# Interleaving projection tiles with sign-product tiles in the last stage of a convolution kernel

## The chip, the cores and the metric

The kernel runs on one core of a Trainium2 chip. The metric is the device time of one execution in microseconds (us), the median of several runs. The engines are named as the profile names them: PE is TensorE (matmuls; PEld are its weight loads), DVE is VectorE, ACT is ScalarE, POOL is GpSimd, SP is SyncE, which here only issues transfers.

## The reference

The input `x` has 384 channels of 192 x 192 pixels in float32. Two layers follow one another, each with a residual. Cut to what matters:

```python
# layer 0
x = x + conv0(gn(x))        # conv0: 1x1 conv to q, k, v; 2x2 max pool; 3x3 depthwise conv;
                            # channel attention (8 heads, four top-k softmaxes); gelu; repeat 2x2;
out = einsum('bchw,oc->bohw', out, w_proj) + b_proj          # the projection, last step of conv0
# layer 1
xb = sign(gn(x)); wb = sign(weight)
shifted = take_along_axis(pad(xb), ...)                      # each channel shifted by -3..3 pixels
x = x + einsum('bchw,oc->bohw', shifted, wb) + bias          # the sign products
```

The normalization of layer 1 needs only the mean of each group of channels, since a sign doesn't depend on the scale. That mean is worked out before the last stage.

## The kernel before, in words

The image is cut into 24 units of 8 rows (`NU`, `UR`). A unit of `x` is a tile `xt` of 128 partitions x 3 channel tiles (`CT`) x 1536 pixels, 2304 KB. Earlier stages take statistics over all units, form q and k and their products, then v, the attention and the gelu; the result for all units lies in six `chunk` tiles of SBUF, at half the resolution in both directions.

The last stage, which starts at line 665, does for each unit, in an order given by the list `order`:

- **The projection**, `projected(ps, u, m)`: for one channel tile `m`, three fp32 matmuls (line 559) of the unit's part of `chunk` by `wpr`, which the profile shows as six passes, into a PSUM tile `yps` (128 x 384); then two additions on DVE (line 568), which add each value to its 2 x 2 pixels of `xt`. `summed(i)` does all three channel tiles of the unit `order[i]`, and issues the load of another unit when a `chunk` tile has been used up.
- **The signs**, `signed(i)`: six sign activations on ACT (line 723; two halves of three channel tiles), each followed by small copies on POOL (`moved`) that shift some channels. The signs lie in one of three fp8 tiles `signs`. In between, ACT issues the store of unit i - 2 (`stored`, line 764), and SP the load of a later unit into the same `xt` (line 768), which waits until that store has landed.
- **The sign products**, `finished(i)`: for each channel tile two PSUM tiles `l1ps` [...], each filled by six fp8 matmuls (line 743) and read by one DVE addition into `xt` (line 751).

PSUM holds two `yps` tiles and three `l1ps` tiles (line 667). The stage runs under `tc.manual_schedule()`: every engine executes its instructions in the order in which the code issues them. The order is the loop at its end:

```python
for i in range(NU):
    if i == 0:
        summed(3)
    elif i > 1 and i + 2 < NU:
        summed(i + 2)
    finished(i)
    if i + 2 < NU:
        signed(i + 2)
```

So in the steps i = 2 to 21, called units below, PE does the three projection tiles of the unit two ahead, and then all six `l1ps` tiles of unit i; DVE does six additions of line 568, then six of line 751.

Of the kernel before, what the change touches and what calls it, by code (L numbers as in the profile page):

```python
# [10 lines left out]
F32 = mybir.dt.float32  # L11
# [5 lines left out]
ALU = mybir.AluOpType  # L17
# [3 lines left out]
P = 128  # L21
C = 384
CT = C // P
# [8 lines left out]
UR = 8  # L32
NU = H // UR
UPX = UR * W
PR = UR // 2
PPX = PR * WP
# [11 lines left out]
SAT = [16 + t * STEP + t - SHIFT // 2 for t in range(CT)]  # L48
# [99 lines left out]
def conv_preact_kernel(ctx: ExitStack, tc: tile.TileContext, a: dict, out: bass.AP):  # L148
    nc = tc.nc
    xv = a["x"].rearrange("u t p n -> u p t n")  # L150
    ov = out.rearrange("u t p n -> u p t n")
# [12 lines left out]
    bpr, bl1, bq, bdw, temp = (parts[i] for i in ("b_proj", "bias", "b_qkv", "b_dw", "temp"))  # L164
# [6 lines left out]
    wb = const.tile([P, CT, C], F8, name="wb")  # L171
# [5 lines left out]
    def unit(u, pool=big, parts=1):  # L177
        xt = pool.tile([P, CT, UPX], F32, name="xt", tag="big")
        n = CT // parts
        for t in range(0, CT, n):  # L180
            nc.sync.dma_start(xt[:, t : t + n], xv[u][:, t : t + n])
        return xt
# [37 lines left out]
    with tc.tile_pool(name="p1", bufs=1, side="right") as p1, tc.tile_pool(name="p1ps", bufs=2, space=PSUM) as psp:  # L220
# [5 lines left out]
        for i in range(NU):  # L226
            u = NU - 1 - i
            xt = unit(u, parts=CT if u in (0, NU - 1) else 1)
# [22 lines left out]
            if u == NU // 2:  # L251

                for m in range(3):
                    ps = psp.tile([NG, C], F32, name="wgps")
# [15 lines left out]
        ps = psp.tile([NG, 2], F32, name="gsps")  # L270
# [10 lines left out]
        ps = psp.tile([P, CT, 2], F32, name="spread")  # L281
# [9 lines left out]
        ps = psp.tile([P, NM], F32, name="bqps")  # L291
# [61 lines left out]
    with tc.tile_pool(name="p2w", bufs=1, side="right") as wp, tc.tile_pool(  # L353
        name="p2t", bufs=2, side="right"
# [65 lines left out]
        for u in range(NU):  # L420
# [4 lines left out]
            xt = kept.pop(u)  # L425
            lo, hi = rows(u)
            n = hi - lo + 1
# [122 lines left out]
    def opened(name, bufs, **kw):  # L550
        return end.enter_context(tc.tile_pool(name=name, bufs=bufs, reuse_waits="tile", **kw))

    def projected(ps, u, m):

        xt = kept[u]
        o = chunk[u // UC][:, :, u % UC * PPX : (u % UC + 1) * PPX]
        x5 = xt.rearrange("p t (i a j b) -> p t a i j b", a=2, b=2, j=WP)
        for t in range(CT):
            nc.tensor.matmul(  # L559
                ps,  # L560
                wpr[:, t, m * P : (m + 1) * P],
                o[:, t, :],
                start=(t == 0),
                stop=(t == CT - 1),
            )
        yb = ps.rearrange("p (i j) -> p i j", j=WP).unsqueeze(3).to_broadcast([P, PR, WP, 2])
        for r in range(2):
            nc.vector.scalar_tensor_tensor(x5[:, m, r], yb, bpr[:, m : m + 1], x5[:, m, r], ALU.add, ALU.add)  # L568

    chunk = []  # L570
    with ExitStack() as vs:
# [34 lines left out]
        for u in range(NU):  # L606
            xt = kept.pop(NU + u) if NU + u in kept else unit(u)
# [9 lines left out]
            for m in range(CT):  # L617
                parts = []
                for c in range(first // CR, last // CR + 1):
                    r0, r1 = max(first, c * CR), min(last, c * CR + CR - 1)  # L620
# [4 lines left out]
                if u == 0 and m == 1:  # L625
                    gathered()
                    po = vs.enter_context(tc.tile_pool(name="p4o", bufs=NP, space=PSUM))
                    psp = vs.enter_context(tc.tile_pool(name="p3ps", bufs=1, space=PSUM))
# [13 lines left out]
        with tc.manual_schedule():  # L642
# [10 lines left out]
            ps = psp.tile([P, P], F32, name="p3ps")[:NG, :1]  # L653
# [4 lines left out]
            ps = psp.tile([P, P], F32, name="p3ps")[:, :CT].unsqueeze(2)  # L658
# [6 lines left out]
    with end:  # L665
        more, sp = opened("p5x1", 1), opened("p5s", 1)
        pyp, psp = opened("p5py", 2, space=PSUM), opened("p5ps", 3, space=PSUM)
        signs = [sp.tile([P, SALL], F8, name=f"signs{i}") for i in range(NSIGN)]

        rest = [sp.tile([P, SLEN], F8, name=f"rest{i}") for i in range(2)]  # L670
        assert SALL % 4 == LEAD % 4 == PITCH % 4 == W % 4 == 0
        for ts in (*signs, *rest):
            nc.gpsimd.memset(ts.bitcast(F32), 0.0)

        def rows_of(ts, p, at=0, pitch=PITCH, n=W):
            return ts[p, at : at + UR * pitch].rearrange("p (r w) -> p r w", w=pitch)[:, :, :n]

        order = [u for c in reversed(range(NCH)) for u in reversed(range(c * UC, (c + 1) * UC))]
        ahead = [*FIRST, NU - 1, *(u for u in order if u // UC == FIRST[0] // UC and u not in FIRST)]
        order = [*ahead, *(u for u in order if u not in ahead)]  # L680
        left = [UC] * NCH
        todo = [u for u in order if u not in kept]

        def summed(i):

            u = order[i]
            if i >= len(FIRST):
                for m in range(CT):
                    projected(pyp.tile([P, PPX], F32, name="yps"), u, m)
            left[u // UC] -= 1  # L690
            if not left[u // UC] and todo:
                v = todo.pop(0)
                kept[v] = unit(v)

        def moved(sg, t, h):

            d, n = OTHER[t][h]
            p = slice(h * HALF + REST, h * HALF + REST + n)
            src, to = SAT[t] - HSHIFT[t][h], SAT[t] - d
            by = rest[t % 2]  # L700
            nc.gpsimd.tensor_copy(
                rows_of(by.bitcast(I32), p, 0, PITCH // 4, W // 4),
                rows_of(sg.bitcast(I32), p, src // 4, PITCH // 4, W // 4),
            )
            if d:

                assert to % 4 == 0
                nc.gpsimd.tensor_copy(sg.bitcast(I32)[p, to // 4 : (to + SLEN) // 4], by.bitcast(I32)[p])
            elif to % 2 == 0:
                nc.gpsimd.tensor_copy(  # L710
                    rows_of(sg.bitcast(U16), p, to // 2, PITCH // 2, W // 2),
                    rows_of(by.bitcast(U16), p, 0, PITCH // 2, W // 2),
                )
            else:
                nc.gpsimd.tensor_copy(rows_of(sg, p, to), rows_of(by, p))  # L715

        def signed(i):

            xt, sg = kept[order[i]], signs[i % NSIGN]
            for k in range(2 * CT):  # L720
                t, h = divmod(k, 2)
                p = slice(h * HALF, (h + 1) * HALF)
                nc.scalar.activation(  # L723
                    rows_of(sg, p, SAT[t] - HSHIFT[t][h]),
                    xt[p, t, :].rearrange("p (r w) -> p r w", w=W),
                    AF.Sign,
                    bias=nmean1[p, t : t + 1],
                    saturate=False,
                )
                moved(sg, t, h)  # L730
                if i > 1 and k == min(2 * (i - 2), CT):
                    stored(i - 2)

        def finished(i):

            u = order[i]
            xt, sg = kept[u], signs[i % NSIGN]
            for m in range(CT):
                for r0 in range(0, UR, 4):
                    ps = psp.tile([P, 2, 512], F32, name="l1ps")  # L740
                    for j in range(2):
                        for t in range(CT):
                            nc.tensor.matmul(  # L743
                                ps[:, j, : 2 * W],
                                wb[:, t, m * P : (m + 1) * P],
                                rows_of(sg, slice(0, P), SAT[t])[:, r0 + 2 * j : r0 + 2 * j + 2],
                                start=(t == 0),
                                stop=(t == CT - 1),
                            )
                    blk = xt[:, m, r0 * W : (r0 + 4) * W].rearrange("p (j n) -> p j n", j=2)  # L750
                    nc.vector.scalar_tensor_tensor(  # L751
                        blk, ps[:, :, : 2 * W], bl1[:, m : m + 1], blk, ALU.add, ALU.add
                    )
                if i + 2 >= NU:
                    nc.sync.dma_start(ov[u, :, m], xt[:, m])

        def stored(i):


            u = order[i]  # L760
            xt = kept.pop(u)
            n = 1 if i < CT else CT
            for t in range(0, CT, n):
                nc.scalar.dma_start(ov[u][:, t : t + n], xt[:, t : t + n])
            if todo:
                v = todo.pop(0)
                for t in range(0, CT, n):
                    nc.sync.dma_start(xt[:, t : t + n], xv[v][:, t : t + n])
                kept[v] = xt

        with tc.manual_schedule():
            v = todo.pop(0)
            kept[v] = unit(v, more, parts=CT)
            for i in range(3):
                summed(i)
                if i < 2:
                    signed(i)
            for i in range(NU):
                if i == 0:
                    summed(3)  # L780
                elif i > 1 and i + 2 < NU:
                    summed(i + 2)
                finished(i)
                if i + 2 < NU:
                    signed(i + 2)

# [71 lines left out]
```

## Time and profile before

| | |
|---|---|
| time, median of 3 runs | 2287.42 us (2287.11 to 2288.5) |
| span of the profiled execution | 2286.9 us |
| PE busy | 2101.7 us, 92% |
| DVE busy | 1903.2 us, 83% |
| ACT busy | 819.4 us, 36% |
| POOL busy | 211.4 us, 9% |
| projection passes in the last stage (line 559 into `yps`) | 396, 136.5 us busy |
| sign products (line 743) | 864, 150.6 us busy |
| additions of line 568 into `xt` from `yps` | 132, 127.9 us busy |
| additions of line 751 | 144, 135.6 us busy |
| signs (line 723) | 144, 226.5 us busy |
| loads into `xt`, 2304 KB each | 12.8 us from issue to landing (median) |
| stores from `xt`, 2304 KB each | 14.4 us from issue to landing (median) |

The profile is of one execution. Busy times are sums over a group of instructions of one line; instructions of one engine overlap at their ends, so that a group's count times the length of one is more than its busy time. In lines of the chain of waits and of the timeline the first number is the start in us from the beginning of the span, the second the length in us, and x12 means twelve instructions joined. A note in brackets, as [0.19 <-DVE xt L568], says how long the engine was idle before and what ended that.

### The profile page before, as it was taken

What the parts mean: (1) busy time and instruction counts of PE and PEld (TensorE: products, weight loads), DVE (VectorE), ACT (ScalarE), POOL (GpSimd) and SP (SyncE); (2) the same over time, 40 slices, a digit from 0 to 9 for tenths busy, and PEclk for the clock granted to TensorE, in tenths of its full rate; (3) what the DMA queues carried; (4) which work ended last, traced back from release to release, by engine and by line L of the source; (5) the groups of instructions that cost most, each with busy time, mean ns of one, the idle gap of its engine ahead of it and who ended that gap; (6) DMA issues with size and microseconds to landing.
All of it is one profiled execution on the core that took longest, in us unless ns stands there. A gap on an engine that the chain in (4) does not pass through costs nothing.

```text
span 2286.9 us, 19474 instructions
## 1 busy us (share of the span) xinstructions
PE 2101.7 (92%) x6135; PEld 993.8 (43%) x6135; DVE 1903.2 (83%) x3269; ACT 819.4 (36%) x1418; POOL 211.4 (9%) x338
## 2 busy tenths in 40 slices
PE   1029999999999999999999979999999999999998
PEld 0014444444444444444444434444444444455554
DVE  4657888888888888888888878986787887889998
ACT  5532222222222222222222212225323233487775
POOL 0000000000000000000000000000000000286674
PEclk7559999999999999999999989999999999999999
DMA  9962222232222232222232222104221212289996
GB/s 398 417 261 60 66 63 70 66 102 69 66 63 71 66 101 70 66 64 70 68 99 70 66 48 83 42 18 189 83 83 67 99 42 83 83 333 404 423 412 248
DMA packets 208727, 300.30 MB, mean 131 GB/s; under 512 B 162000, under 2 KB 164848, under 8 KB 208624
## 3 DMA queue, kind: packets, MB, share of 16 engines
q1 hardware_dynamic: 197936, 243.46, 30.8%
q10 hardware_dynamic: 10688, 55.61, 6.0%
q8 instruction: 48, 0.79, 0.1%
q14 instruction: 55, 0.45, 0.1%
HBM read 213.68 MB, written 56.62 MB: 118 GB/s over the span
## 4 chain that ended last, share of the span: by engine, by line
PE 78%; DVE 11%; DMA 7%; ACT 2%; issue 1%; SPq 1%; ACTq 0%; POOL 0%; POOLq 0%; DVEq 0%
PE qkv L321 65%; DMA xt<-in_x_dram 7%; PE l1ps L743 5%; DVE chunk L344 4%; PE yps L559 3%; PE gram L412 3%; DVE pooled L328 2%; PE ops L594 2%; DVE xt L568 2%; DVE dw L344 1%; DVE stats L248 1%; DMA out_dram<-xt 1%; ACT signs L723 1%; SPq L401 0%; DVE xt L751 0%
## 5 line engine op out<-in xcount | busy, mean ns | idle before, releaser
L321 PE MATMUL qkv<-xt,wq 128*128 128x512 f32 x3888 | 1684.0, 594 | 0.3 <-DVE small L294 0.3
L321 PEld LDWEIGHTS qkv<-xt,wq 128*128 128x128 f32 x3888 | 737.1, 191 | 921.6 <-issue 825.1
L344 DVE SCALAR_TENSOR_TENSOR dw<-pooled,small,dw 128x384 f32<-128x384 f32 (+2 forms) x1152 | 709.2, 616 | 118.8 <-ACT dw L342 93.7
L328 DVE TENSOR_REDUCE pooled<-qkv 128x128 f32<-128x512 f32 x648 | 442.7, 684 | 73.6 <-PE qkv L321 73.1
L344 DVE SCALAR_TENSOR_TENSOR chunk<-pooled,small,chunk 128x384 f32<-128x384 f32 (+3 forms) x696 | 370.5, 546 | 74.7 <-ACT chunk L342 57.3
L346 ACT COPY pooled<-pooled 128x196 f32<-128x196 f32 x207 | 73.7, 356 | 764.5 <-DVE dw L344 543.0
L335 ACT ACTIVATE pooled<-pooled,small 128x384 f32<-128x384 f32 x216 | 133.0, 616 | 409.6 <-DVE pooled L328 402.0
L723 ACT ACTIVATE signs<-xt,nmean 64x1536 fp8e4<-64x1536 f32 x144 | 226.5, 1573 | 61.5 <-PE yps L559 50.3
L743 PE MATMUL l1ps<-signs,wb 128*128 128x384 fp8e4 x864 | 150.6, 329 | 6.2 <-POOL signs L715 4.5
L568 DVE SCALAR_TENSOR_TENSOR xt<-yps,small,xt 128x768 f32<-128x768 f32 x132 | 127.9, 1013 | 23.8 <-PE yps L559 19.6
L559 PE MATMUL yps<-chunk,wpr 128*128 128x384 f32 x396 | 136.5, 490 | 5.5 <-DVE xt L568 5.5
L751 DVE SCALAR_TENSOR_TENSOR xt<-l1ps,small,xt 128x768 f32<-128x768 f32 x144 | 135.6, 1008 | 6.3 <-ACT signs L723 3.6
L248 DVE BATCH_NORM_STATS2 stats<-xt 128x6 f32<-128x512 f32 x144 | 87.2, 675 | 60.4 <-DMA xt<-in_x_dram 60.4
L198 PE MATMUL gsps<-sums,small 128*32 128x2 f32 x6 | 0.5, 196 | 128.5 <-DVE sums L269 128.5
L433 ACT ACTIVATE sq<-dw 128x384 bf16<-128x384 f32 (+2 forms) x144 | 75.3, 523 | 117.0 <-DVE dw L344 117.0
L743 PEld LDWEIGHTS <-wb 128*128 128x128 fp8e4 x864 | 84.1, 97 | 74.0 <-issue 16.3
L302 POOL MEMSET pooled<- 128x196 f32 x9 | 2.4, 265 | 1173.3 <-DVE dw L344 1155.8
L342 ACT ACTIVATE dw<-pooled,small 128x384 f32<-128x384 f32 (+2 forms) x144 | 100.5, 698 | 2.3
L559 PEld LDWEIGHTS yps<-chunk,wpr 128*128 128x128 f32 x396 | 72.6, 190 | 61.0 <-PE yps L559 16.4
L239 ACT ACTIVATE junk<-xt 128x1536 bf16<-128x1536 f32 x48 | 71.1, 1482 | 52.3 <-DMA xt<-in_x_dram 51.1
L383 DVE STREAM_TRANSPOSE blocks<-dw 128x384 f32<-128x384 f32 (+1 forms) x144 | 82.0, 570 | 3.4
L412 PE MATMUL gram<-room 128*128 128x160 f32 (+3 forms) x438 | 68.1, 309 | 15.4 <-DMA room<-blocks 15.4
(117 smaller groups left out, 640.1 us busy)
## 6 DMA issues: line engine op xcount, KB each, us to landing
xt<-in_x_dram SPq DMA_DIRECT2D x83, 2304.0 KB, 12.8
out_dram<-xt ACTq DMA_DIRECT2D x19, 2304.0 KB, 14.4
room<-blocks SPq DMA_DIRECT2D x736, 36.0 KB, 2.0
xt<-in_x_dram SPq DMA_DIRECT2D x18, 768.0 KB, 8.0
out_dram<-xt ACTq DMA_DIRECT2D x9, 768.0 KB, 7.9
out_dram<-xt SPq DMA_DIRECT2D x6, 768.0 KB, 6.6
wq<-in_w_qkvT_dram ACTq DMA_DIRECT2D x1, 1728.0 KB, 15.0
room<-blocks SPq DMA_DIRECT2D x32, 48.0 KB, 2.1
```

The costliest lines, as they stand in the source:

```text
L248: nc.vector.bn_stats(stats[b][:, t, at : at + 6], xt[:, t, j * 512 : (j + 1) * 512])
L321: nc.tensor.matmul(ps, wq[:, t, m * P : (m + 1) * P], x4[:, t, r0 : r0 + nr, c0 : c0 + ncol], start=(t == 0), stop=(t == CT - 1),)
L328: nc.vector.tensor_reduce(pl[:, 2 + r0 // 2 : 2 + (r0 + nr) // 2, 1 + c0 // 2 : 1 + (c0 + ncol) // 2], ps.rearrange("p (i a j b) -> p i j ...
L335: nc.scalar.activation(new, new, AF.Identity, bias=bq[:, m : m + 1])
L342: nc.scalar.activation(acc2, src, AF.Identity, bias=bdw[:, m : m + 1], scale=wdw[:, m, 0:1])
L344: nc.vector.scalar_tensor_tensor(acc2, src, wdw[:, m, k : k + 1], acc2, ALU.mult, ALU.add)
L412: nc.tensor.matmul(gram[t][:, : BN[t] * B], q[:L, t, i], k[:L, B0[t] : B0[t] + BN[t], i], start=u == 0 and i == 0, stop=u == NU - 1 and i ...
L559: nc.tensor.matmul(ps, wpr[:, t, m * P : (m + 1) * P], o[:, t, :], start=(t == 0), stop=(t == CT - 1),)
L568: nc.vector.scalar_tensor_tensor(x5[:, m, r], yb, bpr[:, m : m + 1], x5[:, m, r], ALU.add, ALU.add)
L723: nc.scalar.activation(rows_of(sg, p, SAT[t] - HSHIFT[t][h]), xt[p, t, :].rearrange("p (r w) -> p r w", w=W), AF.Sign, bias=nmean1[p, t : ...
L743: nc.tensor.matmul(ps[:, j, : 2 * W], wb[:, t, m * P : (m + 1) * P], rows_of(sg, slice(0, P), SAT[t])[:, r0 + 2 * j : r0 + 2 * j + 2], sta ...
L751: nc.vector.scalar_tensor_tensor(blk, ps[:, :, : 2 * W], bl1[:, m : m + 1], blk, ALU.add, ALU.add)
```

## The change

`summed` and `finished` are given the channel tile `m`, and the loop calls them in turn: one projection tile of the unit two ahead, then the two `l1ps` tiles of one channel tile of the present unit, and so three times. It is meant to keep PE from waiting for a `yps` tile: with two such tiles, three projection tiles in a row need one of them twice. The instructions and their number are the same; only the order on PE and DVE, and with it the time at which each unit's sums and signs are ready, is another. The first two units and the last two, which have no projection beside them, keep their order. The diff, cut to its core:

```diff
-        def summed(i):
+        def summed(i, m):
             u = order[i]
             if i >= len(FIRST):
-                for m in range(CT):
-                    projected(pyp.tile([P, PPX], F32, name="yps"), u, m)
+                projected(pyp.tile([P, PPX], F32, name="yps"), u, m)
+            if m < CT - 1:
+                return
             left[u // UC] -= 1
...
-        def finished(i):
+        def finished(i, m):
             u = order[i]
             xt, sg = kept[u], signs[i % NSIGN]
-            for m in range(CT):
-                for r0 in range(0, UR, 4):
+            for r0 in range(0, UR, 4):
...
-            for i in range(3):
-                summed(i)
+            for i in range(4):
+                for m in range(CT):
+                    summed(i, m)
                 if i < 2:
                     signed(i)
             for i in range(NU):
-                if i == 0:
-                    summed(3)
-                elif i > 1 and i + 2 < NU:
-                    summed(i + 2)
-                finished(i)
+                for m in range(CT):
+                    if 1 < i < NU - 2:
+                        summed(i + 2, m)
+                    finished(i, m)
                 if i + 2 < NU:
                     signed(i + 2)
```

More of the change, by code (lines that the diff above doesn't have):

```diff
@@ L732, in signed @@
                     stored(i - 2)
-        def finished(i):
+        def finished(i, m):
             u = order[i]
             xt, sg = kept[u], signs[i % NSIGN]
-            for m in range(CT):
-                for r0 in range(0, UR, 4):
[L740 to L755, printed above, removed]
+            for r0 in range(0, UR, 4):
+                ps = psp.tile([P, 2, 512], F32, name="l1ps")
+                for j in range(2):
+                    for t in range(CT):
+                        nc.tensor.matmul(
+                            ps[:, j, : 2 * W],
+                            wb[:, t, m * P : (m + 1) * P],
+                            rows_of(sg, slice(0, P), SAT[t])[:, r0 + 2 * j : r0 + 2 * j + 2],
+                            start=(t == 0),
+                            stop=(t == CT - 1),
+                        )
+                blk = xt[:, m, r0 * W : (r0 + 4) * W].rearrange("p (j n) -> p j n", j=2)
+                nc.vector.scalar_tensor_tensor(
+                    blk, ps[:, :, : 2 * W], bl1[:, m : m + 1], blk, ALU.add, ALU.add
+                )
+            if i + 2 >= NU:
+                nc.sync.dma_start(ov[u, :, m], xt[:, m])
         def stored(i):
```

## The prediction

> **What bounds the kernel now.** I read three views in this order: the span in 40 slices, to find the stage that the change touches; the chain of waits there; the timeline of single engines over one unit. Only the last 300 us matter: the change moves nothing before about 2017 us. The stage's stretches, with busy time (and instructions) of PE, PEld, DVE, ACT and POOL, then clock, DMA share and GB/s:
>
> ```profile
> 2030.00:2083.00 53.00, 50.65 (x224) 28.51 (x223) 46.11 (x49) 41.66 (x27) 37.35 (x54) 1.00 0.95 369
> 2083.00:2255.00 172.00, 168.03 (x753) 94.16 (x751) 159.07 (x168) 131.19 (x84) 116.13 (x168) 1.00 0.92 383
> 2255.00:2287.00 32.00, 22.62 (x122) 12.65 (x120) 22.77 (x25) 12.59 (x8) 11.27 (x16) 0.94 0.72 295
> ```
>
> PE and DVE are both almost always busy, so neither share tells which sets the pace. The chain of waits does (start, us, what):
>
> ```profile
> 2142.78 1.95 PE yps L559 x6
> 2144.75 1.96 DVE xt L568 x2
> 2146.70 0.14 issue
> 2146.84 2.17 PE yps L559 x6
> 2149.01 2.95 PE l1ps L743 x18
> 2151.97 3.11 PE l1ps L743 x18
> 2155.09 1.95 PE yps L559 x6
> 2157.06 1.95 DVE xt L568 x2
> ```
>
> It is a loop that repeats from 2083 to 2267 us. All steps are PE, but for one: after two projection tiles PE must wait until DVE has read the first, because only two `yps` tiles exist. The timeline of PE, then of DVE, in the same unit:
>
> ```profile
> 2142.61 4.03 PE L559 MATMUL yps<-chunk,wpr 128*128 128x384 f32 x12
> 2146.84 2.17 PE L559 MATMUL yps<-chunk,wpr 128*128 128x384 f32 x6 [0.19 <-DVE xt L568]
> 2148.85 6.24 PE L743 MATMUL l1ps<-signs,wb 128*128 128x384 fp8e4 x36
> 2154.92 4.03 PE L559 MATMUL yps<-chunk,wpr 128*128 128x384 f32 x12
> ...
> 2144.75 3.88 DVE L568 SCALAR_TENSOR_TENSOR xt<-yps,small,xt 128x768 f32<-128x768 f32 x4 [0.51 <-PE yps L559]
> 2149.05 1.94 DVE L568 SCALAR_TENSOR_TENSOR xt<-yps,small,xt 128x768 f32<-128x768 f32 x2 [0.43 <-PE yps L559]
> 2150.91 5.63 DVE L751 SCALAR_TENSOR_TENSOR xt<-l1ps,small,xt 128x768 f32<-128x768 f32 x6
> 2157.06 3.88 DVE L568 SCALAR_TENSOR_TENSOR xt<-yps,small,xt 128x768 f32<-128x768 f32 x4 [0.52 <-PE yps L559]
> ```
>
> The period is 2154.92 - 2142.61 = 12.31 us. Three waits of the stage are to be kept in mind (us in all, times, longest):
>
> ```profile
> ACT signs L723 <- PE yps L559: 50.3, 18, 3.8
> PE yps L559 <- DVE xt L568: 5.5, 22, 1.4
> DVE xt L568 <- DMA xt<-in_x_dram: 4.2, 3, 1.9
> ```
>
> [...] the six L751 follow one another at (5.63 - 1.005) / 5 = 925 ns[...] the stage reaches 424 in its busiest stretches.
>
> **The change part by part.**
>
> 1. Bare work of PE per unit. A projection pass takes (4.03 - 0.49) / 11 = 0.322 us (x12, one taking 0.49), so 18 take 5.80. A sign product takes 2.95 / 18 = 0.164, so 36 take 5.90. Together 11.70; the period has 0.61 more. Where: twelve passes should end at 2142.61 + 3.87 = 2146.48, and the thirteenth starts at 2146.84 (0.36); its six last 2148.85 - 2146.84 = 2.01 and not 1.93 (0.08); the 36 products last 2154.92 - 2148.85 = 6.07 (0.17). The last loss lies between products 18 and 19 (the second 18 take 3.11, not 2.95): product 19 opens the fourth `l1ps` tile, whose buffer DVE frees when its first L751, begun at 2150.91, is through.
>
> 2. What the new order removes. It alternates one projection tile (1.93) with two `l1ps` tiles (1.97): 3.90 us per channel tile. The `yps` tile needed next was filled two channel tiles (7.8 us) earlier, and in the built program the later projections carry no wait at all. DVE needs 2 x 0.934 + 2 x 0.925 = 3.72 for the same channel tile, less than PE, so it lags by one tile's work and no more: the first L751 of a channel tile ends about 5 us after that channel tile's start on PE, and its buffer is wanted again three `l1ps` tiles later, at about 7. So all of 0.61 should go: PE's period becomes 11.70.
>
> 3. What it adds. Six changes between fp32 and fp8 per unit in place of two. Before shows each kind once per unit: from the last projection pass to the first product 0.32, from the last product to the first pass 0.16, each no more than the instruction itself. I take zero; the upper bound is 0.08 (the restart of step 1) for four more, 0.3. For DVE a wait at each of six changes: an L568 that starts after idling costs some 0.08 more (it takes 1.018 where the next follows after 0.934); 3.72 + 0.08 is still under 3.90. What stands behind a waiting DVE instruction is the next pair of additions, and PE has two to three filled tiles of room.
>
> 4. What moves: the third projection tile of unit i+2 is added by DVE about 4 us later. Signs of channel tile 2 stand on ACT behind the store of unit i, which waits for the last L751 of unit i anyway; signs of tile 1 have their input 6 us into the unit, and ACT comes to them at about 7 (0.5 for the store's issue, then four signs of 1.6). ACT does six signs (9.44) per unit and waits 2.75, so about 2 of slack remain. The products need the signs a unit later. Chunk buffers are freed by PE 4 us later, but the two loads I checked (2029.28 and 2071.20) stood in SP's queue behind another load until 3 us and more after that. Cost: nothing, hidden in ACT's and SP's waiting.
>
> 5. How many units. Units 2 to 7 run while the DMA engines are full (share 0.99 to 1.01 but for 2045 to 2060, where it is 0.83): loads set the pace, DVE waiting for `xt` at units 3, 4 and 7. The new order helps at unit 3: DVE waited 1.9 us there for the last third of a load with sum and product of the first thirds undone, and now does these first. Its store is issued up to 1.9 us earlier, into the slack stretch, and the loads that follow may gain as much. After the last stall (2083.21) DVE takes 11.2 instead of 12.3 us for unit 7, as PE has run ahead. Between 0.9 and 3.0; I take 2.0.
>
> 6. From the first projection addition of unit 8 (2095.52) to that of unit 21 are 13 periods: 13 x 0.61 = 7.9. The last addition of unit 21 comes 0.2 sooner within its unit. The tail (signs and products of the last two units, last stores) is the same. Sum 2.0 + 7.9 + 0.2 = 10.1; 2287.4 - 10.1 = 2277.3 us.
>
> **The rivals.**
>
> A, the above: 2277.3, chance 0.56.
>
> B, PE doesn't get all: the 0.17 and 0.08 stay in another form, or changes of type cost up to 0.3 per unit. Period 11.95 to 12.05: 13 x 0.3 = 3.9, with 1.5 from the early units: 5.4, so 2282.0. For it: only two changes per unit were ever seen, and DVE has 0.1 us of slack per channel tile. Against it: those two cost nothing. 0.24.
>
> C, the loads take over. One unit moves 4.72 MB, at 424 GB/s 11.13 us, only 0.57 under the new period, and chunk buffers bring two more loads between 2110 and 2175. Should the loads hold the pace at 12.31 until they end at about 2225, the gain is some five units of 0.61 and one of unit 7: 4, so about 2283.4 to 2286. Against it: load for unit 8's projection lands, by the bytes of the load queue, at about 2092, needed at 2094.5; three units later the slack is 9 us and grows. 0.14.
>
> D, slower: the later signs become the bound. If ACT's chain (store issue, two signs, wait for tile 1, two signs, wait for the store) took 0.25 longer than a period of 12.31, 20 units would lose 5: 2292. Against it: 2 us of slack, worked out in 4. 0.06.
>
> **How the numbers follow.** A is the likeliest: 2277.3. Below it only the 3.0 of step 5 lies and some luck: 2275.5. Above, the range takes in B and the near end of C: 2283.0. C's rest (0.08) and D (0.06) stay out, with a little of A's lower side. Faster by over 0.2% means under 2282.8: A, three quarters or more of B, a little of C, 0.80; slower is D, 0.06; same the rest, 0.14.
>
> **What would show it.** Right: PE's timeline shows 6 passes, 12 products, 6 passes, with no idle note from DVE; the period from 2095 on is 11.7; the entry "PE yps <- DVE xt" shrinks from 22 times to none or a few; DVE's waits for PE become many short ones. B: period of 12 with PE idle put down to issue or DVE. C: more than three DVE waits for `xt` loads. D: PE or PEld waiting for ACT signs or POOL beyond the three of before. Wrong altogether: the period stays at 12.3, which would mean that PE's bare work is more than 11.70.

## The result, and the profile after

| | before | after |
|---|---|---|
| time, median of 4 runs | 2287.96 us (2287.11 to 2289.1) | 2275.48 us (2274.21 to 2276.92) |
| ratio, 95% interval | | 0.9945 [0.9928, 0.9963] |
| span of the profiled execution | 2286.9 us | 2274.4 us |

The change takes 12.5 us away. The forecast was 10.1, and the time lies 0.02 us below the low end of its range. Single executions of after lie between 2274.2 and 2276.9, so that on which side of that end their median falls is chance; what has to be explained is the 2.4 us between 10.1 and 12.5. The interval of the ratio alone (a gain of 8.5 to 16.5 us) can't tell these two apart; the traces, unit by unit, can. The chain of waits of after, in a unit of the same stretch as shown for before (start, length, what):

```profile
2141.77 1.97 PE l1ps L743 x12
2143.73 1.94 PE yps L559 x6
2145.67 1.97 PE l1ps L743 x12
```

There is nothing but PE in it: the steps "issue" and "DVE xt" are gone. PE's timeline of after, then DVE's:

```profile
2139.67 2.10 PE L559 MATMUL yps<-chunk,wpr 128*128 128x384 f32 x6
2141.60 2.13 PE L743 MATMUL l1ps<-signs,wb 128*128 128x384 fp8e4 x12
2143.57 2.10 PE L559 MATMUL yps<-chunk,wpr 128*128 128x384 f32 x6
...
2149.41 2.13 PE L743 MATMUL l1ps<-signs,wb 128*128 128x384 fp8e4 x12
2151.38 2.10 PE L559 MATMUL yps<-chunk,wpr 128*128 128x384 f32 x6
...
2141.80 1.94 DVE L568 SCALAR_TENSOR_TENSOR xt<-yps,small,xt 128x768 f32<-128x768 f32 x2
2143.66 1.94 DVE L751 SCALAR_TENSOR_TENSOR xt<-l1ps,small,xt 128x768 f32<-128x768 f32 x2
2145.71 1.94 DVE L568 SCALAR_TENSOR_TENSOR xt<-yps,small,xt 128x768 f32<-128x768 f32 x2
```

A unit lasts 2151.38 - 2139.67 = 11.71 us in place of 12.31. No line of PE carries an idle note. DVE starts the two additions of a projection tile every 3.91 us (2145.71 - 2141.80) and is idle for some 0.1 of it. The waits of after (engine, tile and line, what it waited for: us in all, times, longest):

```profile
ACT signs L724 <- PE yps L559: 23.6, 11, 2.1
PE l1ps L743 <- POOL signs L716: 4.8, 2, 3.5
DVE xt L568 <- DMA xt<-in_x_dram: 4.7, 2, 2.6
DVE xt L568 <- PE yps L559: 2.8, 5, 0.9
PE yps L559 <- DVE xt L568: 0.4, 2, 0.2
```

PE's wait for a free `yps` went from 22 times and 5.5 us to twice and 0.4. ACT's wait for projections halved (50.3 to 23.6 us): with PE quicker, the slack of ACT is smaller but still there. DVE's waits for loads are 4.7 us as against 4.2; what of them reaches PE is told below.

**Where the 12.5 us lie.** Unit 1's last addition ends at 2018.0 us in both traces (2018.01 and 2018.06). From there, by DVE's timelines (the first row gives a moment, the others lengths, all in us):

| stretch | before | after | gain | forecast |
|---|---|---|---|---|
| up to the first projection addition of unit 8, at | 2095.52 | 2091.82 | 3.7 | 2.0 |
| from there to that of unit 21 | 160.00 | 151.46 | 8.5 | 7.9 |
| from there to the end of unit 21 | 11.8 | 11.6 | 0.2 | 0.2 |
| from the end of unit 21 to the end of the kernel | 19.55 | 19.55 | 0 | 0 |

In this pair of traces, then, the early units gave nearly twice what the forecast put down. How that looks on DVE, in after, around the last wait for a load:

```profile
2069.41 1.94 DVE L568 SCALAR_TENSOR_TENSOR xt<-yps,small,xt 128x768 f32<-128x768 f32 x2 [2.55 <-DMA xt<-in_x_dram]
2071.27 1.93 DVE L751 SCALAR_TENSOR_TENSOR xt<-l1ps,small,xt 128x768 f32<-128x768 f32 x2
...
2080.71 1.94 DVE L568 SCALAR_TENSOR_TENSOR xt<-yps,small,xt 128x768 f32<-128x768 f32 x2
...
2091.82 1.93 DVE L568 SCALAR_TENSOR_TENSOR xt<-yps,small,xt 128x768 f32<-128x768 f32 x2
...
2102.92 1.94 DVE L568 SCALAR_TENSOR_TENSOR xt<-yps,small,xt 128x768 f32<-128x768 f32 x2
```

Unit 6 begins at 2069.41 after a stall of 2.55 us. The next three units start 11.30, 11.11 and 11.10 later each: DVE's own pace (12 additions of 0.925 are 11.10), below PE's 11.71. PE had filled tiles ahead during the stall, and for some three units DVE works these off. In before, units 5 and 6 and all from 8 on took 12.31 from end to end (unit 4, 12.41). There PE could not stay ahead, since it waited for DVE once per unit.

How much of a stall reaches PE, which sets the pace, can be read from PE's lines. In after, behind DVE's stalls of 2.19 us (at 2044) and 2.55 us:

```profile
2046.19 2.44 PE L743 MATMUL l1ps<-signs,wb 128*128 128x384 fp8e4 x12
2072.33 1.15 PE L743 MATMUL l1ps<-signs,wb 128*128 128x384 fp8e4 x6 [1.26 <-DVE xt L751]
```

Twelve products last 2.13 elsewhere, so that the first stall cost PE 0.3; the second cost 1.26 of idling and the 0.16 by which products otherwise overlap the matmul before them (2.13 against the 1.97 of the chain), 1.4 together. In before, DVE's stalls were 1.88, 0.62 and 1.70, and PE's notes are these, where an undisturbed unit has 0.19 in the place of the last two:

```profile
2039.91 3.12 PE L743 MATMUL l1ps<-signs,wb 128*128 128x384 fp8e4 x18 [1.46 <-DVE xt L751]
2047.19 2.17 PE L559 MATMUL yps<-chunk,wpr 128*128 128x384 f32 x6 [0.29 <-DVE xt L568]
2085.30 2.17 PE L559 MATMUL yps<-chunk,wpr 128*128 128x384 f32 x6 [1.38 <-DVE xt L568]
```

So in before a stall came through to PE but for some 0.4 or 0.5 us (1.46 of 1.88, 0.10 of 0.62, 1.19 of 1.70); in after, 1.1 and 1.9 us did not come through. In all, waits for loads cost PE 2.7 us in before and 1.7 in after, and the lengths of units 2 to 20 give the same two sums. The new order thus takes up a part of each stall.

What the DMA engines did meanwhile, in the stretches 2018 to 2078 and 2083 to 2245 (from:to, length, busy of PE, PEld, DVE, ACT, POOL, then clock, DMA share and GB/s), of after:

```profile
2018.00:2078.00 60.00, 58.59 (x270) 33.88 (x269) 53.70 (x59) 52.22 (x34) 46.60 (x67) 1.00 0.96 378
2083.00:2245.00 162.00, 162.00 (x751) 94.51 (x750) 158.12 (x168) 131.60 (x84) 115.87 (x168) 1.00 0.97 403
```

and of before:

```profile
2018.00:2078.00 60.00, 57.45 (x256) 32.06 (x255) 53.26 (x58) 51.15 (x34) 45.26 (x65) 1.00 0.95 360
2083.00:2245.00 162.00, 158.23 (x705) 88.50 (x703) 149.50 (x158) 123.49 (x80) 107.96 (x157) 1.00 0.95 396
```

In the early stretch the share hardly moved (0.95 to 0.96), and yet 5% more was carried (360 to 378 GB/s). Before alone shows the same already, in two stretches with a share of 1.01 and 1.02:

```profile
2071.00:2083.30 12.30, 12.10 (x55) 6.79 (x54) 10.18 (x12) 9.48 (x7) 8.29 (x12) 1.00 1.01 386
2107.80:2120.10 12.30, 12.10 (x55) 6.78 (x55) 11.37 (x12) 9.44 (x6) 8.30 (x12) 1.00 1.02 424
```

So a share near 1 stood beside 386 GB/s and beside 424 alike, and didn't show how much was still to be had. From 2083 to 2245 PE of after is busy all of the time.

### The profile page after: what moved, and what is told of

It is laid out like the page before. It is cut to its first block, busy times and chain, and to the rows that moved or that the text cites. A ratio compares the mean times of both kernels' runs of the same rounds, so it can differ in the third digit from the quotient of the medians.

```text
span 2274.4 us, 19469 instructions
## 1 busy us (share of the span) xinstructions
PE 2093.8 (92%) x6135; PEld 995.7 (44%) x6135; DVE 1902.4 (84%) x3269; ACT 819.4 (36%) x1418; POOL 211.3 (9%) x338
## 4 chain that ended last, share of the span: by engine, by line
PE 79%; DVE 11%; DMA 6%; ACT 2%; issue 1%; SPq 1%; ACTq 0%; POOL 0%; POOLq 0%; DVEq 0%
PE qkv L321 64%; PE l1ps L743 6%; DMA xt<-in_x_dram 5%; PE yps L559 5%; DVE chunk L344 5%; PE gram L412 3%; DVE pooled L328 2%; PE ops L594 2%; DVE dw L344 1%; DVE stats L248 1%; ACT signs L724 1%; ACT chunk L342 0%; ACT pooled L335 0%; SPq L401 0%; DVE xt L751 0%
## 5 line engine op out<-in xcount | busy, mean ns | idle before, releaser
L724 ACT ACTIVATE signs<-xt,nmean 64x1536 fp8e4<-64x1536 f32 x144 | 226.5, 1573 | 49.0 <-PE yps L559 23.6
```

The costliest lines, as they stand in the source:

```text
L724: nc.scalar.activation(rows_of(sg, p, SAT[t] - HSHIFT[t][h]), xt[p, t, :].rearrange("p (r w) -> p r w", w=W), AF.Sign, bias=nmean1[p, t : ...
```

## The experiments

Each is a small edit of the last stage. Medians are given with the ratio to the kernel before and its 95% interval; "gain" is the difference from the median of before on the same chip (2287.6 to 2288.1). Single executions of one kernel differ by 2 us and more: in the traces, unit 1 ends between 2015.7 and 2018.1 us (but for the kernel with one `yps` tile), before most of the edits have any effect, and the early waits for loads scatter too.

**Which units gave it.** The alternation is kept only where `c` holds; elsewhere the three projection tiles go first as before:

```diff
-                for m in range(CT):
-                    if 1 < i < NU - 2:
-                        summed(i + 2, m)
-                    finished(i, m)
+                ahead = i + 2 if 1 < i < NU - 2 else None
+                if ahead and not c:
+                    for m in range(CT):
+                        summed(ahead, m)
+                for m in range(CT):
+                    if ahead and c:
+                        summed(ahead, m)
+                    finished(i, m)
```

`c` is `i > 7` in the first, `i < 8` in the second, `i == 3` in the third and `4 <= i < 8` in the fourth.

Late units alone:

> Alternates from unit 8 on only; units 2 to 7 keep the old order. Theory (two separate gains: 0.6 us in each steady unit from PE's waits for PSUM tiles, and some 3.7 us in the load-paced units 2 to 7): unit 8 begins where it began before (first projection addition at about 2095.5 us), period 11.7 from there, gain 8.0 to 8.5, so about 2279.3. Rival (the steady units are the whole gain, the early 3.7 being chance in the transfers): about 2275.5, as the full change.

Early units alone:

> Alternates in units 2 to 7 only; from unit 8 on the old order. Theory: first projection addition of unit 8 at about 2091.8 us, then periods of 12.3; gain 3.7, so about 2284. Rival (all of the gain in the steady units): no gain, 2287.5. The two gains of this run and of the one with the late units should add up to the 12.4 us of the full change.

Unit 3 alone, the prediction's own reason for the gain before unit 8:

> Alternates in unit 3 only. If the early gain comes from unit 3 alone (DVE no longer idles 1.9 us for the last third of a load, its store goes out 2 us sooner): 3 to 3.7 us gained by unit 8, about 2284. If it comes from the load-paced units together, each issuing its store somewhat sooner: 0.5 to 1.5 gained, about 2286.5.

Units 4 to 7 alone:

> Alternates in units 4 to 7 only, that is without units 2 and 3. Theory A (after a wait for a load, DVE, which needs only 11.1 us per unit, catches up with PE, which has run ahead into the PSUM tiles; that happens in units 4 to 7 alone): nearly the whole early gain, 3 to 3.5 us, about 2284.5. Theory B (each of the six units simply saves 0.6 us, the loads following suit): 4 x 0.6 = 2.4, about 2285.6. The prediction's own reason (unit 3's earlier store): nothing, 2288.

| alternating in | median us | ratio | gain |
|---|---|---|---|
| units above 7 | 2279.79 | 0.9963 [0.9951, 0.9976] | 8.3 |
| units below 8 | 2284.6 | 0.9986 [0.9979, 0.9993] | 3.5 |
| unit 3 | 2288.07 | 1.0002 [0.9994, 1.001] | 0 |
| units 4 to 7 | 2285.08 | 0.9988 [0.998, 0.9996] | 2.9 |

The two halves come out at 8.3 and 3.5, near what the traces of before and after had (8.5 + 0.2 and 3.7), and add up to 11.8 of the 12.5. The interval of the early half is wide: 1.6 to 4.8 us. By itself it doesn't exclude the 2.0 of the forecast. The traces help here: from the end of unit 1 to that of unit 7, the two with the old order in these units (before and the kernel with late units alone) take 77.0 and 78.0 us; the three with the new order (after, early units alone, and the kernel at the end of this section that stores unit 21 by channel tile) take 73.9, 74.9 and 74.5. Every one of the three is more than 2.0 us below either of the two, and the means lie 3.1 apart. After unit 7, another 0.6 and more comes in while DVE still catches up.

Unit 3 alone gives nothing in its median (interval -2.3 to 1.4 us). In its trace, its store went out earlier by some 1.6 to 2 us, but half of that went into a new wait at unit 4 (1.43 us), and the wait at unit 7 stayed (1.69, in before 1.70). So the reason that step 5 gave for most of its term, unit 3 and the loads behind its store, is not the cause. Units 4 to 7 alone bring 2.9 (interval 0.9 to 4.6), which lies between what the two theories of that run expected and doesn't decide between them; it does show a gain in these units, which the forecast held to be paced by loads.

**Which wait was removed.** Two projection tiles, then four `l1ps` tiles, then the third projection tile, then two `l1ps` tiles:

```diff
-                    if 1 < i < NU - 2:
-                        summed(i + 2, m)
+                    if ahead and m != 1:
+                        for k in (0, 1) if m == 0 else (2,):
+                            summed(ahead, k)
                     finished(i, m)
```

> All units from 2 to 21, but in the order two projection tiles, two channel tiles of sign products, one projection tile, one channel tile of products. Theory (only a third projection tile in a row has to wait, as there are two yps tiles): no wait for yps, the period at most 0.1 us over 11.7, so 2275.5 to 2277. Rival (PE and DVE must alternate tile by tile to keep step): part of the 0.6 us comes back, a period near 12, about 2280.

2280.4 us, 0.9966 [0.9954, 0.9979]: a gain of 7.7, not the full one that was expected; the time is the one that the rival of that run named, but with a shorter period than its "near 12". PE's timeline of this kernel has no wait for `yps`:

```profile
2146.32 2.10 PE L559 MATMUL yps<-chunk,wpr 128*128 128x384 f32 x6
2148.26 2.13 PE L743 MATMUL l1ps<-signs,wb 128*128 128x384 fp8e4 x12
2150.23 4.03 PE L559 MATMUL yps<-chunk,wpr 128*128 128x384 f32 x12
2154.10 4.27 PE L743 MATMUL l1ps<-signs,wb 128*128 128x384 fp8e4 x24
2158.20 2.10 PE L559 MATMUL yps<-chunk,wpr 128*128 128x384 f32 x6
```

Its period is 2158.20 - 2146.32 = 11.88. The chain of waits shows the 0.17 that stayed:

```profile
2142.38 2.95 PE l1ps L743 x18
2145.34 0.01 issue
2145.34 1.15 PE l1ps L743 x6
```

18 products take 2.95, so six take 0.98, and the six after the break, which open the fourth `l1ps` tile, take 1.15. This splits the 0.60 us per unit (12.31 - 11.71): 12.31 - 11.88 = 0.43 was the wait for `yps` with its restart, 11.88 - 11.71 = 0.17 the wait for the fourth `l1ps` tile in a row. The change removes both.

The change with one `yps` tile in place of two:

```diff
-        pyp, psp = opened("p5py", 2, space=PSUM), opened("p5ps", 3, space=PSUM)
+        pyp, psp = opened("p5py", 1, space=PSUM), opened("p5ps", 3, space=PSUM)
```

> The full change with one yps tile in place of two: the wait that the change removed, put back. A projection tile can then begin only when DVE has read the last one, 2.13 + 1.87 + 0.15 = 4.15 us after that began, against 3.90: period 12.45, 0.15 over the old order's, so about 2289. If the wait for yps were not what the change removed, the time would stay at 2275.5.

2314.79 us, 1.0113 [1.01, 1.0127]: 26.9 us slower than before, where about 2289 had been expected. The chain of waits of this kernel, and a line of PE's timeline:

```profile
2154.99 2.19 PE yps L559 x6
2157.18 0.03 issue
2157.20 1.95 DVE xt L568 x2
2159.16 0.14 issue
2159.29 2.19 PE yps L559 x6
...
2154.99 2.17 PE L559 MATMUL yps<-chunk,wpr 128*128 128x384 f32 x6 [0.16 <-DVE xt L568]
```

The tile is filled (2.19), read by DVE (1.95), and the hand-overs cost 0.03 and 0.14: 4.30 us per channel tile, 12.90 per unit. The two `l1ps` tiles that stand between fit into the reading and cost nothing. 4.15 had been expected; each part came out a little longer than put down (2.19 for 2.13, 1.95 for 1.87, 0.17 for 0.15). The two profiled executions lie 22.7 us apart, and this is where: unit 1 ends 8.7 later than in before, since six projection tiles go in a row ahead of unit 0's products; unit 2 takes 18.16 in place of 12.71; and the 19 units from 3 on take 12.90 each, 245.1 in place of 236.6. The last term would be 11 but for before's waits for loads, of which this kernel has none. The expectation had counted the period alone. The other 4 us of the medians are in no trace.

The change with two `l1ps` tiles in place of three, by the same line (3 to 2):

> The full change with two l1ps tiles in place of three. The steady period stays 11.7, since with alternation a buffer is wanted again 3.9 us after it was filled and DVE is through with it after about 3.2. PE can run ahead of a DVE that waits for a load by one tile (1 us) less: theory A loses some 0.5 to 1 us of the early gain, 2276 to 2276.5; theory B loses nothing, 2275.5. If the third tile were needed in the steady units: period over 12, 2280 or more.

2275.78 us, 0.9948 [0.9934, 0.9961], the same as the change; the period in its trace is 11.71. With one `yps` tile the period of the alternation was 12.90, with two it is 11.71, and here the third `l1ps` tile brought nothing (one alone was not tried). The loss that one theory expected from a smaller lead of PE was not seen in the time, but at 0.5 to 1 us it would hide in the spread of these runs (2274.1 to 2277.4). PE's idle notes fit a smaller lead: behind DVE's stalls of 1.80 and 1.05 us, PE idled 0.74 and 0.38 here.

**What the loads took.** In both orders, a load that follows a store brings only channel tile 0 of its unit; two thirds of these loads are left out:

```diff
-                for t in range(0, CT, n):
-                    nc.sync.dma_start(xt[:, t : t + n], xv[v][:, t : t + n])
+                nc.sync.dma_start(xt[:, :1], xv[v][:, :1])
```

In the order of before:

> The old order, but a load that follows a store brings only the first of three channel tiles (the output is then not that of the reference; the work of the engines is the same). No DVE wait for a load: units 2 to 7 at 12.3 like the others, 73.9 us from the end of unit 1 to that of unit 7 in place of 77.0; about 2285, the loads' waits costing 3 us in the old order.

In the order of the change:

> The full change with the same light loads (the same part is left out). Units 2 to 7 at 11.7: 70.3 us to the end of unit 7. Theory (the waits for loads cost about as much in either order, as loads follow stores and stores follow the units): 12 us less than the old order with light loads, about 2273, and 2.5 to 3 less than the full change. The prediction's reading (units 2 to 7 are paced by the DMA engines, so that the new order gains only a part of its 0.6 there): the waits would cost more in the new order, 4.5 or more, about 2271 or less.

2285.04 us, 0.9986 [0.998, 0.9993], for the old order and 2273.33 us, 0.9934 [0.9922, 0.9946], for the new. In neither trace does DVE wait for a load in this stage; unit 2 takes 12.7 in both, and every unit from 3 to 21 takes 12.31 or 11.71. The two medians differ by 11.7 us; 19 units of 0.60 are 11.4. With whole loads they differ by 12.5. So loads cost 3.0 us in the old order (2288.0 - 2285.0) and about 2.2 in the new (2275.5 - 2273.3, from two chips); by the traces, 2.7 and 1.7. They took nothing of the gain, where the prediction's reading would have had them cost 4.5 or more in the new order. This is what the forecast had wrong.

**Stores, the order within a pair, and the end.** The products of a channel tile before the projection tile:

```diff
-                        summed(i + 2, m)
                     finished(i, m)
+                    if 1 < i < NU - 2:
+                        summed(i + 2, m)
```

> Alternates, but the products of a channel tile go ahead of the projection of the same channel tile. The period is the same 11.7; loads get 2 us more before they are needed, the last unit's signs come 2 us later, so that the tail's wait for them grows by 1 to 2. Together 2275 to 2277. If the order within a pair mattered for the steady units (DVE waiting longer for PE): 2278 or more.

2273.55 us, 0.9934 [0.9922, 0.9947]: 1.9 under the change, at the same period of 11.71, and below the 2275 to 2277 expected. Its waits have one for a load, not two:

```profile
DVE xt L568 <- DMA xt<-in_x_dram: 1.5, 1, 1.5
```

Whether this comes from the store, which is ready one projection tile sooner, was tried by putting that store behind the signs of the next two units, products first as above:

```diff
-                if i > 1 and k == min(2 * (i - 2), CT):
+                if i > 1 and k == (2 * CT - 1 if i > 4 else min(2 * (i - 2), CT)):
```

> Products first, as in the run before, but the store of a unit is issued behind all six signs, not behind the fourth: some 5 us later. Theory (the time at which a unit's store is issued sets when the load behind it lands, and so the waits for loads): 5 to 8 us of new waits in units 4 to 10, 2279 to 2282. If the moment of the store doesn't matter, the DMA engines being full anyway: 2273.5 as before.

2275.03 us, 0.9944 [0.9932, 0.9957], not the 2279 to 2282 expected. The stores went out 1.2 to 2.6 us later, not 5, and unit 7 ended as soon as without the edit (71.15 and 71.19 us after unit 1). What is lost (1.5 in the medians, 2.3 in this part of the traces) is lost behind unit 21, whose store is late too: 21.81 us are left from there to the end, and 19.55 with products first. A store's moment, by some 2 us, set no load's wait here.

The last stage's end was tried next: products first up to unit 20, projection first for unit 21, whose store alone goes behind the signs.

```diff
-                if i > 1 and k == min(2 * (i - 2), CT):
+                if i > 1 and k == (2 * CT - 1 if i == NU - 1 else min(2 * (i - 2), CT)):
...
+                    if ahead == NU - 1:
+                        summed(ahead, m)
                     finished(i, m)
+                    if ahead and ahead < NU - 1:
+                        summed(ahead, m)
```

> Products first in units 2 to 20, projection first in unit 21, and in the last signs the store behind the sixth sign, so that the last unit's signs come 2 us sooner. The tail's waits of PE (1.0) and DVE (0.8) before the last products go: about 2272.7, 0.8 under products first throughout. If the tail waits for something else: 2273.5.

2275.03 us, 0.9943 [0.993, 0.9955]: the 2272.7 expected was missed by 2.3. The last additions came 1.2 us sooner than in the kernel with products first, and yet the end came later (1.5 in the medians, 1.75 in the traces), as the store of unit 21 went out later. The issue of that store here:

```profile
2252.80 0.38 ACTq L764 DMA_DIRECT2D out_dram<-xt  x1
```

and with products first:

```profile
2251.05 0.38 ACTq L764 DMA_DIRECT2D out_dram<-xt  x1
```

From 2252.80 on the DMA engines of this kernel are busy to the end while PE is not (columns as above):

```profile
2252.80:2269.80 17.00, 10.08 (x62) 5.72 (x60) 11.13 (x12) 1.40 (x1) 2.84 (x4) 0.91 0.96 393
```

17 us at 393 GB/s are 6.7 MB: nearly all of the three units that are then still to be stored (7.1 MB). And from the end of unit 21 to the end of the kernel it is 19.55 or 19.56 us with products first, here, and in the change, though the last addition comes 14.3, 11.2 and 12.6 us after unit 21. Behind unit 21, then, transfers set the end, not signs and products. In the change the DMA engines idle half of the time just before (first line) and are full after (second):

```profile
2243.00:2255.00 12.00, 11.99 (x62) 6.88 (x61) 11.67 (x14) 9.44 (x6) 8.36 (x13) 1.00 0.49 198
2255.00:2272.00 17.00, 10.15 (x61) 5.70 (x59) 11.27 (x12) 3.15 (x2) 2.98 (x4) 0.93 0.97 396
```

So unit 21 was stored by channel tile, each as soon as it is through, as the last two units already are:

```diff
-                if i > 1 and k == min(2 * (i - 2), CT):
+                if 1 < i < NU - 1 and k == min(2 * (i - 2), CT):
...
-            if i + 2 >= NU:
+            if i + 3 >= NU:
                 nc.sync.dma_start(ov[u, :, m], xt[:, m])
```

> The full change, but unit 21 is stored like the last two units: by channel tile on SP's queue, each as soon as its last addition is done, instead of whole on ACT's. Theory T (the tail is set by three stores that begin only when unit 21 is done: 7.1 MB at full rate, 19.6 us from the end of unit 21 to the end of the kernel in every run that stores unit 21 there): two thirds of one store leave earlier, and the last signs no longer stand behind it: 15.2 to 17 us, so 2272 to 2273. Rival (the prediction's picture: the tail is the last unit's signs, products and additions): signs 2 us sooner, about 1 us gained, 2274.5.

2271.4 us, 0.993 [0.9917, 0.9942]: 4.1 under the change. From the end of unit 21 to the end of the kernel there are 15.59 us in place of 19.55. The edit also takes the store out of ACT's queue, so that the last signs, products and additions come sooner (the last addition 11.2 us after unit 21); the kernel tried just ahead of this one had that as well and gained nothing behind unit 21, which leaves the earlier pieces of the store. The two stretches of this kernel:

```profile
2245.00:2257.00 12.00, 11.99 (x64) 6.83 (x64) 11.78 (x14) 10.45 (x7) 10.07 (x15) 1.00 0.84 342
2257.00:2270.00 13.00, 7.13 (x44) 3.99 (x42) 8.19 (x9) 0.00 (x0) 0.70 (x1) 0.90 0.87 355
```

342 GB/s are now moved beside the last full unit, where it was 198. This edit, together with the order of the kernel ahead of it (products first, projection first for unit 21), has the lowest median:

> Products first in units 2 to 20, projection first in unit 21, and unit 21 stored by channel tile on SP's queue. Theory T: the sooner end of the last products, which brought nothing while the stores set the tail, now counts: about 29.5 us from the end of unit 20 to the end, against 31.3 with products first throughout, 2271.5 to 2272. Rival: nothing over products first throughout, 2273.5, or worse.

2270.68 us, 0.9928 [0.9915, 0.9942], 17.0 under before and 4.8 under the change, and a little below the 2271.5 to 2272 expected. Its 0.7 us over the kernel with that edit alone is within the spread of the two (2270.1 to 2272.7). No wait for a load is left in the early units of its trace, where the two other traces with the same early order have one, of 1.5 and 1.85 us: that is scatter of single executions. 15.55 us remain behind unit 21.

## Why the prediction was wrong, point by point

- **Step 1, bare work of 11.70 and 0.61 of losses: right.** The period is 11.71. The split was right as well (0.36 + 0.08 and 0.17 in the forecast): 0.43 with `yps`, 0.17 with the fourth `l1ps` tile, told apart by the order in pairs.
- **Step 2, all of 0.61 goes: right.** Rival B's period of 11.95 to 12.05 didn't come.
- **Step 3, changes of type at nothing: right.** Six changes a unit are in the 11.71, which is 0.01 over 18 passes and 36 products. DVE's small waits were there as said, about 0.1 per channel tile, too short for the view of waits to list. One reading in this step is not what the lines show: an addition takes 1.005 to 1.02 us whether DVE was idle before or not, and starts 0.925 to 0.934 after the one before when nothing holds it up. No part of the forecast hung on it.
- **Step 4, later signs and chunk frees at nothing: right.** ACT still waited 23.6 us for projections; PE's two waits for signs made by POOL (4.8 us in all) stand at 2009 and 2260 us, outside the alternating units, and before has the same two (4.5 us). Rival D fell.
- **Step 5, the failed step.** It held that in units 2 to 7 "loads set the pace" and so put down 2.0 for them, from unit 3's earlier store and a quicker unit 7. The gain up to unit 8 is 3.7 in the traces and 3.5 in the run with those units alone. The reading behind the term, "the DMA engines are full (share 0.99 to 1.01 ...)", was wrong: only three stalls of DVE lay in that stretch, they cost 2.7 us in all, and the other units but for the first took the 12.31 of PE's period. What the step gave as the reason for a gain was refuted in its main part (unit 3 alone: 0). What it had in one place only, that DVE catches up after a stall because PE has run ahead, happens behind each stall in the new order: units 4, 6, 7 and 8 of after took 11.10 to 11.30. In place of the term stand two things. The units from 3 on save their 0.60 like all others, and waits for loads cost PE about 1.0 less than in before, not more. Rival C made the same mistake more strongly; the thinned loads settle it.
- **Step 6, 13 periods at 7.9: 8.5 measured.** 13 x 0.60 are 7.8; the rest is that unit 8 and part of 9 still ran at DVE's 11.10, working off what PE had filled during unit 6's stall. The step had granted that only to unit 7.
- **Step 6, the tail the same: right in size, incomplete in cause.** 19.55 us in both. The step named signs, products and last stores; the runs show that the stores set it, from the moment that unit 21 is done and its store goes out.

In sum, counted from end to end of a unit: 0.1 in unit 2, 19 units x 0.60 = 11.4, and 1.0 because loads' waits cost 1.7 in place of 2.7, against 12.5 measured. The forecast counted 13 units in full, 0.2 for unit 21, and the six before unit 8 at 2.0 together. Its 0.61 per unit, its largest term, was sound.

**Still open.** Why the loads landed hardly later although the units ran quicker: DVE's own waits for them grew from 4.2 to 4.7 us only. It is seen that the DMA engines carried more in the same stretch (360 to 378 GB/s), not why. That stalls reach PE more weakly in the new order is read from the lines of the traces (in the kernel that stores unit 21 by channel tile, too, DVE's 2.75 and 2.76 us left PE idle for 0.78 and 1.48); no run was made to vary it alone. Why products first has shorter waits for loads is open too: the moment of the store was ruled out as far as 2 us of delay go, and that a load is needed about 2 us later in this order was not tried by itself.

## What to carry to other kernels

Here two groups of matmuls, each with a small ring of PSUM tiles (the few tiles that it uses in turn), followed one another on PE, and alternating them at the size of one tile ended both rings' waits, 0.43 and 0.17 us of a unit's 12.31, with no more memory. In a kernel built like it, count the tiles filled in a row against the ring, for each ring. Before writing off a stretch as paced by loads, sum what the waits for them cost the engine that sets the pace (2.7 us here), and look at the length of the units between: here those had the period of the compute chain, 12.31 us, and a quicker chain was worth its whole difference, 0.60 per unit. At the end, what wasn't yet stored when the compute was nearly done set the finish here, and storing it in smaller pieces, each as soon as it was finished, took 4 us off.

## What the runs showed of the hardware that wasn't expected

- A share of busy DMA engines near 1 came with 360, 378, 396 and 403 GB/s in stretches of the same kind of traffic (shares 0.95 to 0.97), and in before alone with 386 and 424 (shares 1.01 and 1.02); the share alone didn't tell what was left.
- Alternating six fp32 passes with twelve fp8 products, six changes a unit, cost nothing: 11.71 us against 18 x 0.322 + 36 x 0.164 = 11.70.
- The one `yps` tile that was filled and read in strict turn cost, beside its filling (2.19 us) and its reading (1.95), 0.03 us from PE to DVE, 0.14 back, and 0.07 for PE's restart (six passes last 2.17 in PE's timeline, in after 2.10).
- In the new order PE went on filling tiles while DVE waited for a load: DVE's stalls of 2.19 and 2.55 us cost PE 0.3 and 1.4; in the old order, one of 1.88 cost 1.46.
